# Layer 0's output projection by channel and transposed back, and its variance products spread over the MLP

## The chip, the cores and the metric

The kernel runs on one core of a Trainium2 chip. Its time is the time on the device in microseconds (us), as the median of several runs. A profile was taken of one more run. It gives for every instruction the engine, the start and the length. The engines are named as in the profile: PE is TensorE's matmul, PEld its weight load, DVE is VectorE, ACT is ScalarE, POOL is GpSimd, SP issues transfers.

## The reference, cut to what matters

The network has two layers on an image of 64 x 64 positions ("tokens") with 96 channels. Each layer is a state-space mixer with a residual, then an MLP with a residual whose values are rounded to 8-bit and 16-bit floats. The change lies where layer 0 ends. There the scan's result `y` (4096 tokens, 192 channels) is normalised over its channels, gated, projected to 96 channels and added to `x`; then comes the MLP. The tail of layer 0, with gain 1 and bias 0 of the normalisation in these inputs:

```python
y = layernorm(y, eps=1e-5) * ln_g + ln_b      # over the 192 channels of a token
y = y * silu(z)
x = x + y @ out_proj_w                        # 192 -> 96 channels, per token
# MLP
t = layernorm(x, eps=1e-5)
h = relu(q16(q8(t) @ q8(W1).T) + q8(b1))      # 96 -> 384 (each sum rounded to 16 bits)
x = x + (q16(q8(h) @ q8(W2).T) + q8(b2))      # 384 -> 96
# layer 1 begins
xn = layernorm(x, eps=1e-6);  xz = xn @ W_in.T ...
```

Since the factor 1/sqrt(variance) of a token is the same for all its channels, the kernel applies it after the projection, when it adds the result to the residual.

## The kernel before: the parts concerned

The tokens are cut into 8 chunks of 512. `res` holds the residual with tokens on the partitions (128 x 4 tokens x 96 channels of a chunk). `y` lies with channels on the partitions: `y[0]` has channels 0 to 127 of all tokens, `y[1]` has channels 128 to 191 of one chunk on partitions 0 to 63 and of another on 64 to 127 (the two `LANES`). So the work goes in turns `s` of two chunks, software-pipelined: turn `s` prepares the centred `y` of turn `s + 1`, finishes the mixer and runs the MLP for turn `s`, and hands the chunks of turn `s - 1` to layer 1.

```python
for s in range(-1, n + 1):                    # n = 4
    if s + 1 < n:
        self.centred(s + 1, chunks(s + 1))
    if 0 <= s < n:
        self.gated_out(s, chunks(s))
    for c in chunks(s - 1):
        self.to_layer1(c)
    for c in chunks(s - 1):
        self.keep_in_proj(c)
    if s + 1 < n:
        self.variance(s + 1, chunks(s + 1))
    for c in chunks(s):
        self.mlp_turn(0, c)
    for c in chunks(s):
        self.mlp_up(0, c)
    for c in chunks(s):
        self.mlp_down(0, c)
        self.xn[c] = self.norm_chunk(self.lp, c, self.eps6, F32, f"c{c}")
```

`keep` fixes an instruction's place: it stays behind all that was written before it for the same engine. All TensorE products here are kept, so TensorE works in the order of the program. What isn't kept on VectorE, ScalarE and GpSimd is put in order by the scheduler when the kernel is built. Each engine then works its own list in order.

```python
def centred(self, s, chunks):                 # subtract the mean over the channels
    m = [self.pa.tile([P, CH], F32, tag="a", name=f"m{c}") for c in chunks]
    for t, c in zip(m, chunks):
        keep(nc.tensor.matmul(t, self.mean, y0[:, chunk(c)], start=True, stop=False))
    for t, r in zip(m, LANES):
        keep(nc.tensor.matmul(t, self.mean[r], y1[r, chunk(s)], start=False, stop=True))
    ...                                       # y -= mean (VectorE), sq = y*y (ScalarE),
                                              # y *= silu(z) (GpSimd)

def variance(self, s, chunks):                # sum of squares over the channels, both chunks
    v = self.po.tile([2, CH], F32, tag="o", name=f"ov{s}")
    for i, sq in enumerate(self.sq.pop(s)):
        self.keep(nc.tensor.matmul(v, self.rows[i], sq, start=i == 0, stop=i == 2))
    sd = self.lp.tile([2, CH], F32, tag="osd", name=f"osd{s}")
    nc.scalar.activation(sd, v, AF.Sqrt, bias=self.eps5[0:2])
    r = self.lp.tile([P, 2, 4], F32, tag="or", name=f"or{s}")
    for k in range(2):
        nc.sync.dma_start(r[:, k], sd[k : k + 1].rearrange("k (p j) -> k p j", j=4))
    nc.vector.reciprocal(r, r)
    ...                                       # self.factor[c] = r[:, k]

def gated_out(self, s, chunks):
    for c in chunks:
        o = self.po.tile([P, 4, CD], F32, tag="o", name=f"o0{c}")
        self.out_proj(o, self.y, self.wg, c, self.keep)
        for j in range(4):
            to, r = self.res[:, c, j, :], self.factor[c][:, j : j + 1]
            nc.vector.scalar_tensor_tensor(to, o[:, j, :], r, to, ALU.mult, ALU.add)
        self.mlp_norm(0, c)

def out_proj(self, t, y, w, c, keep):         # L596 and L597 in the profile
    ...
    for j in range(4):                        # y stationary (128 tokens), w moves (96 columns)
        at = [slice(k * CH + j, (k + 1) * CH, 4) for k in (c, s)]
        keep(nc.tensor.matmul(t[:, j, :], y[0][:, at[0]], w[0], start=True, stop=False))
        keep(nc.tensor.matmul(t[:, j, :], y[1][r, at[1]], w[1][r], start=False, stop=True))

def to_layer1(self, c):                       # 4 transposes (L188), a ScalarE copy, a transfer
def keep_in_proj(self, c):                    # 2 products of 512 columns (L331), 2 copies
def mlp_norm(self, li, c):                    # normalise on VectorE/ScalarE, round to 8 bits,
                                              # POOL widens to bf16: xb
def mlp_turn(self, li, c):                    # 4 transposes of xb (L188), a ScalarE copy: xt
def mlp_up(self, li, c):                      # for m in 0, 1, 2:
    ...
        a = self.ph.tile([P, CH], F32, tag="h", name=f"h{li}{c}{m}")
        self.keep(nc.tensor.matmul(a, w1[:, m * P : (m + 1) * P], xt, start=True, stop=True))
        ...                                   # ScalarE copies to 16 bits, ScalarE (m = 0) or
                                              # VectorE adds b1 and clamps, POOL rounds to 8 bits
def mlp_down(self, li, c):                    # 12 products of 96 columns, then into res
```

PSUM tiles come from small pools: `a` has 3 buffers (means, input projection), `o` has 2 (out_proj, the variance, the MLP's second product), `h` has 2 (the MLP's first product), `t` has 1 (transposes).

Of the kernel before, what the change touches and what calls it, by code (L numbers as in the profile page):

```python
# [28 lines left out]
F32 = mybir.dt.float32  # L29
# [5 lines left out]
ALU = mybir.AluOpType  # L35
# [4 lines left out]
P = 128  # L40
# [3 lines left out]
CD = 96  # L44
# [4 lines left out]
CH = 512  # L49
# [44 lines left out]
LANES = (slice(0, 64), slice(64, 128))  # L94
# [12 lines left out]
def chunk(c):  # L107
    return slice(c * CH, (c + 1) * CH)
# [12 lines left out]
class Net:  # L121
# [897 lines left out]
    def back0(self):  # L1019

        tc = self.tc
        self.xn_d = self.scratch("xn1", [CD, L])
        with ExitStack() as ctx:
            self.tp = ctx.enter_context(tc.tile_pool(name="af0", bufs=3))
            self.lp = ctx.enter_context(tc.tile_pool(name="al0", bufs=2))
            self.pa = ctx.enter_context(tc.tile_pool(name="ps_a0", bufs=3, space=PSUM))  # L1030
            self.po = ctx.enter_context(tc.tile_pool(name="ps_o0", bufs=2, space=PSUM))
            self.ph = ctx.enter_context(tc.tile_pool(name="ps_h0", bufs=2, space=PSUM))
            self.pt = ctx.enter_context(tc.tile_pool(name="ps_t0", bufs=1, space=PSUM))
            self.w_in = self.w_in1
            n = NCH // 2
            self.sq, self.factor, self.xb, self.xn, self.xt, self.hid = {}, {}, {}, {}, {}, {}

            def chunks(s):
                c0 = s // 2 * 4 + s % 2
                return (c0, c0 + 2) if 0 <= s < n else ()  # L1040

            for s in range(-1, n + 1):
                if s + 1 < n:
                    self.centred(s + 1, chunks(s + 1))
                if 0 <= s < n:
                    self.gated_out(s, chunks(s))
                for c in chunks(s - 1):
                    self.to_layer1(c)
                for c in chunks(s - 1):
                    self.keep_in_proj(c)  # L1050
                if s + 1 < n:
                    self.variance(s + 1, chunks(s + 1))
                for c in chunks(s):
                    self.mlp_turn(0, c)
                for c in chunks(s):
                    self.mlp_up(0, c)
                for c in chunks(s):
                    self.mlp_down(0, c)
                    self.xn[c] = self.norm_chunk(self.lp, c, self.eps6, F32, f"c{c}")

    def keep(self, instruction):
        self.tc.keep_in_program_order(instruction)
# [20 lines left out]
    def variance(self, s, chunks):  # L1083

        nc = self.nc
        v = self.po.tile([2, CH], F32, tag="o", name=f"ov{s}")
        for i, sq in enumerate(self.sq.pop(s)):
            self.keep(nc.tensor.matmul(v, self.rows[i], sq, start=i == 0, stop=i == 2))
        sd = self.lp.tile([2, CH], F32, tag="osd", name=f"osd{s}")
        nc.scalar.activation(sd, v, AF.Sqrt, bias=self.eps5[0:2])  # L1090
        r = self.lp.tile([P, 2, 4], F32, tag="or", name=f"or{s}")
# [3 lines that stand above are left out]
        for k, c in enumerate(chunks):  # L1095
            self.factor[c] = r[:, k]

    def gated_out(self, s, chunks):

        nc = self.nc  # L1100
        for c in chunks:
            o = self.po.tile([P, 4, CD], F32, tag="o", name=f"o0{c}")
            self.out_proj(o, self.y, self.wg, c, self.keep)
            for j in range(4):
                to, r = self.res[:, c, j, :], self.factor[c][:, j : j + 1]
                nc.vector.scalar_tensor_tensor(to, o[:, j, :], r, to, ALU.mult, ALU.add)
            self.mlp_norm(0, c)

    def to_layer1(self, c):
        nc = self.nc  # L1110
# [855 lines left out]
        self.to_channels(t, self.xb.pop(c), self.identb, xt, "c (j p) -> c j p", self.keep)  # L1966
        self.xt[c] = xt

    def mlp_up(self, li, c):

        nc = self.nc
        w1, w2, b1, b2 = self.mlp_w[li]
        xt = self.xt.pop(c)
        self.hid[c] = []
        for m in range(HID // P):
            a = self.ph.tile([P, CH], F32, tag="h", name=f"h{li}{c}{m}")
            self.keep(nc.tensor.matmul(a, w1[:, m * P : (m + 1) * P], xt, start=True, stop=True))
            h16 = self.tp.tile([P, CH], F16, tag="h16", name=f"h16{li}{c}{m}")
            nc.scalar.copy(h16, a)
            if m == 0:  # L1980
                nc.scalar.activation(h16, h16, AF.Relu, bias=b1[:, m : m + 1])
            else:
                nc.vector.tensor_scalar(h16, h16, b1[:, m : m + 1], 0.0, ALU.add, ALU.max)
            h8 = self.tp.tile([P, CH], FP8, tag=f"h8{m}", name=f"h8{li}{c}{m}")
            nc.gpsimd.tensor_copy(h8, h16, saturate=False)
            self.hid[c].append(h8)
# [100 lines left out]
```

## Time and profile before

| | us |
|---|---|
| time, median of 3 runs (lowest to highest) | 1490.06 (1487.32 to 1494.84) |
| span of the profiled run | 1489.0 |
| PE busy | 1186.5 (80%) |
| DVE busy | 1155.5 (78%) |
| ACT busy | 907.6 (61%) |
| POOL busy | 784.6 (53%) |
| out_proj of layer 0, 128 records on PE | 48.6 |
| variance products, 24 records on PE | 13.5 |

Such a table says how much each engine works over the whole span, and it can mislead here: the kernel is a row of stages with different limits. The changed functions run in one stretch of some 160 us near the beginning, once per chunk or once per turn, and long before the stretch in which layer 1's scans keep VectorE busy. What a change in them is worth has to be read from that stretch: which engine works without a gap there, and what the others wait for. A product of f32 operands appears in the records as two matmuls (and two weight loads), one of 8-bit or 16-bit operands as one. The ends of matmuls are modelled, so the distance between the starts of two is the better measure of what one costs. The clock that a view gives for TensorE is the granted share of its full speed.

### The profile page before, as it was taken

The numbers are of one execution on the slowest core, as the hardware profiler recorded it, in microseconds if no ns is written. First come the engines' busy times: TensorE is split into PE (matmuls) and PEld (weight loads), VectorE is DVE, ScalarE is ACT, GpSimd is POOL, SyncE is SP. The second block draws the span as 40 slices with busy tenths as digits, with TensorE's granted clock in tenths as the row PEclk, the third lists the DMA queues.
The fourth block names the chain that finished last, engine by engine and source line by source line (L and its number), as shares of the span: only waits on it lengthen the run. The fifth ranks groups of instructions, "written<-read, shape, count | busy, mean of one in ns | idle before, by whom it ended". The sixth has DMA issues, their size and how long they took to land. (4 is left out here: it accounts for less than half of the span.)

```text
span 1489.0 us, 13012 instructions
## 1 busy us (share of the span) xinstructions
PE 1186.5 (80%) x4040; PEld 496.6 (33%) x4040; DVE 1155.5 (78%) x887; ACT 907.6 (61%) x1091; POOL 784.6 (53%) x461
## 2 busy tenths in 40 slices
PE   7998887799996377677777677787777888899975
PEld 4533444243332122222222222222222343344343
DVE  6493455303337999999999999999999999999875
ACT  3454333304446677677777777777777777777434
POOL 1002221100001687778777877777778777875545
PEclk8998566799998688888888888988888898987865
DMA  2143000003317745645555454635364557342201
GB/s 63 53 136 66 11 10 13 11 24 87 81 36 208 244 135 180 215 138 159 180 162 183 137 183 151 203 113 194 123 227 132 171 171 248 122 150 72 87 0 43
DMA packets 68851, 183.21 MB, mean 123 GB/s; under 512 B 21488, under 2 KB 35460, under 8 KB 61956
## 3 DMA queue, kind: packets, MB, share of 16 engines
q1 hardware_dynamic: 67480, 182.00, 39.3%
q8 instruction: 34, 0.56, 0.2%
q10 hardware_dynamic: 1292, 0.28, 0.1%
q14 instruction: 45, 0.37, 0.1%
HBM read 155.98 MB, written 20.47 MB: 118 GB/s over the span
## 5 line engine op out<-in xcount | busy, mean ns | idle before, releaser
L1552 POOL TENSOR_TENSOR hss<-h1s,xws 128x1024 f32<-128x1024 f32 x96 | 224.6, 2377 | 132.0 <-PE hs L1560 131.4
L1536 ACT ACTIVATE da<-dt1s,a 128x1024 f32<-128x1024 f32 x168 | 187.9, 1118 | 147.9 <-DVE xws L1547 87.5
L1560 PE MATMUL hs<-hss,ident 128*128 128x512 f32 x376 | 212.0, 647 | 59.4 <-DMA dt<-dtc 33.5
L1547 DVE TENSOR_TENSOR_SCAN xws<-da,xws 128x1024 f32<-128x1024 f32 x96 | 224.1, 2335 | 10.4 <-DVE xws L1547 2.7
L1536 ACT ACTIVATE da<-dt0s,a 128x1024 f32<-128x1024 f32 x168 | 187.2, 1114 | 68.4 <-DVE xws L1547 52.2
L1560 PE MATMUL hs<-h0s,ident 128*128 128x512 f32 x376 | 199.1, 612 | 0.0
L1547 DVE TENSOR_TENSOR_SCAN h1s<-da,h1s,xws 128x1024 f32<-128x1024 f32 x72 | 169.2, 2350 | 10.4 <-ACT da L1536 1.3
L1560 PEld LDWEIGHTS hs<-hss,ident 128*128 128x128 f32 x376 | 68.6, 200 | 193.4 <-issue 75.9
L1375 POOL TENSOR_TENSOR dun<-u,dtn 128x512 f32<-128x512 f32 x4 | 5.9, 1482 | 197.8 <-DVE dtn L1272 107.6
L1560 PEld LDWEIGHTS hs<-h0s,ident 128*128 128x128 f32 x376 | 74.1, 198 | 97.2 <-issue 92.4
L1581 PE MATMUL acc<-hc2s,fold 128*32 128x512 f32 x128 | 47.1, 825 | 61.0 <-POOL hc2s L1570 58.0
L1581 PE MATMUL acc<-hc0s,fold 128*32 128x512 f32 x128 | 46.2, 809 | 52.6 <-POOL hc0s L1570 52.6
L1581 PE MATMUL acc<-hc1s,fold 128*32 128x512 f32 x128 | 46.5, 815 | 50.1 <-POOL hc1s L1570 50.1
L1520 POOL TENSOR_TENSOR x1s<-x1s,dus 128x1024 f32<-128x1024 f32 x32 | 75.0, 2361 | 8.8 <-DMA x1s<-bc 8.8
L1520 POOL TENSOR_TENSOR x2s<-x2s,dus 128x1024 f32<-128x1024 f32 x32 | 75.3, 2369 | 6.9 <-DMA c1s<-bc 6.9
L1547 DVE TENSOR_TENSOR_SCAN x0s<-da,x0s 128x1024 f32<-128x1024 f32 x32 | 74.7, 2335 | 4.3 <-ACT da L1536 2.0
L1547 DVE TENSOR_TENSOR_SCAN x1s<-da,x1s 128x1024 f32<-128x1024 f32 x32 | 74.7, 2335 | 3.5 <-ACT da L1536 0.9
L1547 DVE TENSOR_TENSOR_SCAN x2s<-da,x2s 128x1024 f32<-128x1024 f32 x32 | 74.7, 2335 | 3.4 <-ACT da L1536 0.8
L1560 PE MATMUL hs<-x0s,ident 128*128 128x512 f32 x128 | 66.7, 603 | 0.2 <-DVE x0s L1547 0.2
L1560 PE MATMUL hs<-x1s,ident 128*128 128x512 f32 x128 | 66.6, 602 | 0.0
L1520 POOL TENSOR_TENSOR x0s<-x0s,dus 128x1024 f32<-128x1024 f32 x28 | 65.8, 2363 | 0.0
L1232 PE MATMUL cv<-pad,cw 128*128 128x512 f32 x144 | 64.3, 598 | 0.0
(343 smaller groups left out, 2423.1 us busy)
## 6 DMA issues: line engine op xcount, KB each, us to landing
c0s<-bc SPq DMA_DIRECT2D x184, 128.0 KB, 2.6
c1s<-bc SPq DMA_DIRECT2D x184, 128.0 KB, 2.6
x2s<-bc SPq DMA_DIRECT2D x32, 512.0 KB, 4.8
x0s<-bc SPq DMA_DIRECT2D x28, 512.0 KB, 3.8
x1s<-bc SPq DMA_DIRECT2D x28, 512.0 KB, 6.2
dus<-du SPq DMA_DIRECT2D x20, 512.0 KB, 6.7
dt1s<-dt SPq DMA_DIRECT2D x40, 256.0 KB, 6.6
dt0s<-dt SPq DMA_DIRECT2D x40, 256.0 KB, 4.6
```

What stands on the lines that cost most here:

```text
L1232: keep(nc.tensor.matmul(t, cw[0][:, tap, 0:P], v, start=tap == 0, stop=False))
L1375: keep(nc.gpsimd.tensor_tensor(dun, u[1][:, m], dtn, ALU.mult))
L1520: keep(nc.gpsimd.tensor_tensor(x, x, du[:, part[j]], ALU.mult))
L1536: keep(nc.scalar.activation(das[i, s], dts[o][:, part[j]], AF.Exp, scale=self.a6[:, g, k : k + 1]))
L1547: keep(nc.vector.tensor_tensor_scan(to, da, x, start, ALU.mult, ALU.add))
L1552: keep(nc.gpsimd.tensor_tensor(cols(hs)[:, w, :], grid(h1)[:, w, :], grid(xw)[:, w, :], ALU.add))
L1560: keep(nc.tensor.matmul(t, self.ident, x[:, chunk(m)], start=x is hs, stop=x is xs[i % 3]))
L1581: keep(nc.tensor.matmul(to, self.fold4, src, start=k == 0, stop=k == NK - 1))
```

## The change

`gated_out` used `y` as the stationary operand: for each 128 tokens it loaded 128 columns of `y` and moved only the 96 columns of the weights through the array. Now the weights are stationary, and 512 tokens move in one product. The result then has channels on the partitions. ScalarE copies it out of PSUM, and four transposes per chunk bring it back to tokens, where the factor is applied as before. The layer-1 transposes of the turn before are put between the two chunks' transposes. The second part concerns the variance of the next turn: its three products no longer stand in one block ahead of the MLP. One comes before the MLP, and one in each chunk's `mlp_up` ahead of the last of three products. The MLP's transposes and first products go chunk by chunk, where both chunks were transposed first before.

```diff
                 if 0 <= s < n:
-                    self.gated_out(s, chunks(s))
-                for c in chunks(s - 1):
-                    self.to_layer1(c)
+                    self.gated_sums(s, chunks(s))
+                for k in range(2):
+                    for c in chunks(s - 1)[k : k + 1]:
+                        self.to_layer1(c)
+                    for c in chunks(s)[k : k + 1]:
+                        self.gated_out(c)
                 for c in chunks(s - 1):
                     self.keep_in_proj(c)
-                if s + 1 < n:
-                    self.variance(s + 1, chunks(s + 1))
+                sums = self.variance(s + 1, chunks(s + 1)) if s + 1 < n else iter(())
+                next(sums, None)
                 for c in chunks(s):
                     self.mlp_turn(0, c)
-                for c in chunks(s):
-                    self.mlp_up(0, c)
+                    self.mlp_up(0, c, lambda: next(sums, None))
+                for _ in sums:
+                    pass
...
         for i, sq in enumerate(self.sq.pop(s)):
             self.keep(nc.tensor.matmul(v, self.rows[i], sq, start=i == 0, stop=i == 2))
+            if i < 2:
+                yield
...
+    def gated_sums(self, s, chunks):
+        nc, keep = self.nc, self.keep
+        o = [self.ph.tile([P, CH], F32, tag="h", name=f"oc{c}")[0:CD] for c in chunks]
+        for t, c in zip(o, chunks):
+            keep(nc.tensor.matmul(t, self.wg[0], self.y[0][:, chunk(c)], start=True, stop=False))
+        for t, r in zip(o, LANES):
+            keep(nc.tensor.matmul(t, self.wg[1][r], self.y[1][r, chunk(s)], start=False, stop=True))
+        self.ot = {}
+        for t, c in zip(o, chunks):
+            self.ot[c] = self.lp.tile([CD, CH], F32, tag="ot", name=f"ot{c}")
+            nc.scalar.copy(self.ot[c], t)

-    def gated_out(self, s, chunks):
+    def gated_out(self, c):
         nc = self.nc
-        for c in chunks:
-            o = self.po.tile([P, 4, CD], F32, tag="o", name=f"o0{c}")
-            self.out_proj(o, self.y, self.wg, c, self.keep)
-            for j in range(4):
-                ...
-            self.mlp_norm(0, c)
+        o = self.po.tile([P, 4, CD], F32, tag="o", name=f"o0{c}")
+        by_token = self.ot[c].rearrange("c (p j) -> c j p", j=4)
+        for j in range(4):
+            self.keep(nc.tensor.transpose(o[:, j, :], by_token[:, j, :], self.ident[0:CD, 0:CD]))
+        for j in range(4):
+            ...                               # as before
+        self.mlp_norm(0, c)
...
-    def mlp_up(self, li, c):
+    def mlp_up(self, li, c, between=lambda: None):
...
         for m in range(HID // P):
+            if m == 2:
+                between()
```

More of the change, by code (lines that the diff above doesn't have):

```diff
@@ L1096, in variance @@
             self.factor[c] = r[:, k]
-    def gated_out(self, s, chunks):
-        nc = self.nc
-        for c in chunks:
-            o = self.po.tile([P, 4, CD], F32, tag="o", name=f"o0{c}")
-            self.out_proj(o, self.y, self.wg, c, self.keep)
-            for j in range(4):
-                to, r = self.res[:, c, j, :], self.factor[c][:, j : j + 1]
-                nc.vector.scalar_tensor_tensor(to, o[:, j, :], r, to, ALU.mult, ALU.add)
-            self.mlp_norm(0, c)
+    def gated_sums(self, s, chunks):
[10 more added lines that the diff above has]
+    def gated_out(self, c):
+        nc = self.nc
+        o = self.po.tile([P, 4, CD], F32, tag="o", name=f"o0{c}")
[3 more added lines that the diff above has]
+        for j in range(4):
+            to, r = self.res[:, c, j, :], self.factor[c][:, j : j + 1]
+            nc.vector.scalar_tensor_tensor(to, o[:, j, :], r, to, ALU.mult, ALU.add)
+        self.mlp_norm(0, c)
     def to_layer1(self, c):
```

## The prediction

> **What bounds the kernel now.** I first asked where the change sits in the span: the rows of its lines place it between 124.6 and 284.6 us of 1489, in the stretch where layer 0 is finished and its MLP runs. From the page's slices, each 37.2 us, the clock row matters most here:
>
> ```profile
> PE   7998887799996377677777677787777888899975
> PEclk8998566799998688888888888988888898987865
> ```
>
> The fifth to seventh slices (149 to 261 us) have TensorE 70 to 80% busy at 0.5 to 0.7 of its clock, the lowest in the kernel. Then I cut the stretch at the starts of its pipeline turns, in the windows view (us, busy time and number of records of PE, PEld, DVE, ACT, POOL, then clock, DMA share, GB/s):
>
> ```profile
> 133.80:164.30 30.50, 25.20 (x85) 13.47 (x85) 12.91 (x31) 10.81 (x21) 9.32 (x12) 0.69 0.04 6
> 164.30:202.10 37.80, 31.60 (x103) 17.09 (x102) 18.71 (x44) 14.13 (x28) 8.73 (x11) 0.68 0.04 11
> 202.10:240.10 38.00, 31.56 (x103) 17.12 (x102) 18.74 (x44) 14.12 (x28) 8.74 (x11) 0.68 0.04 11
> 240.10:270.60 30.50, 23.97 (x89) 14.96 (x87) 16.21 (x39) 11.76 (x24) 4.78 (x8) 0.61 0.06 14
> 284.60:400.00 115.40, 115.40 (x480) 41.56 (x480) 27.02 (x42) 36.88 (x52) 2.54 (x2) 1.00 0.21 58
> ```
>
> The first four rows are turns s = 0 to 3. No engine but TensorE is busy even half of a turn, and it is busy 83% of it. The last row is layer 1's convolution, which begins when the last turn's input projection is copied: TensorE is busy in every microsecond of it, so whatever the turns lose or win moves the rest of the kernel by as much. Next, the inside of turn 1, cut at its steps: the means, out_proj, the transposes to layer 1, its input projection, the variance, the wait for the normalised rows, and the MLP:
>
> ```profile
> 164.30:169.70 5.40, 5.40 (x11) 1.67 (x9) 3.25 (x8) 1.82 (x4) 0.00 (x0) 0.52 0.02 3
> 169.70:180.80 11.10, 11.10 (x35) 8.69 (x33) 5.02 (x12) 1.56 (x3) 2.53 (x2) 0.64 0.00 0
> 180.80:183.20 2.40, 1.73 (x9) 1.25 (x9) 1.92 (x6) 1.11 (x2) 0.12 (x1) 0.50 0.00 0
> 183.20:188.40 5.20, 5.20 (x10) 2.12 (x8) 1.54 (x3) 2.27 (x5) 1.14 (x1) 0.68 0.26 76
> 188.40:191.10 2.70, 2.70 (x7) 0.42 (x6) 1.99 (x6) 0.63 (x2) 0.67 (x1) 1.00 0.00 0
> 191.10:194.30 3.20, 0.65 (x8) 0.47 (x8) 1.06 (x3) 1.34 (x3) 0.51 (x1) 1.00 0.04 1
> 194.30:202.10 7.80, 4.82 (x34) 2.46 (x33) 3.93 (x8) 5.39 (x10) 3.76 (x6) 0.66 0.00 0
> ```
>
> out_proj is the largest step, 11.1 us, and weight loads are 8.7 us of it. Up to 191 TensorE has no gap over 1 us: it sets the time. From 191 on it waits on others, first for normalised rows (0.65 of 3.20 us busy), then for the MLP's copies. Last, single rows of the timeline (start, length, engine, line, shapes):
>
> ```profile
> 164.33 3.75 PE L1070 MATMUL m<-y,mean 128*128 128x512 f32 x4
> 168.01 1.82 PE L1072 MATMUL m<-y,mean 64*128 64x512 f32 x4
> 169.75 0.71 PE L596 MATMUL o<-wg,y 128*128 128x96 f32 x2
> 175.08 0.78 PE L596 MATMUL o<-wg,y 128*128 128x96 f32 x2
> 180.76 1.09 PE L188 MATMUL tr<-ident,lnxnc 128*96 128x128 f32 x4
> 188.47 2.74 PE L1088 MATMUL ov<-sq,rows 128*2 128x512 f32 x6
> 194.11 0.42 PE L188 MATMUL tf<-identb,xb 128*96 128x128 bf16 x4 [2.55 <-POOL xb L1960]
> ```
>
> One f32 product is two records. Two out_proj records start every 0.64 us at the beginning and every 0.71 us later, after the clock has fallen: it is bound by the loads, not by the stream. A transpose is one record of 0.27 us. A 512-column record takes 0.85 us at the half clock (the variance of turn 0: six in 5.05 us) and 0.43 at the full one (six here in 2.67 us). The last row: the second chunk's turn waits 2.55 us for POOL, while the first chunk could already go through the MLP.
>
> **What the Trainium skill says.** "TensorE: Matmul & The Clock Gate", Part 1: the clock is halved by default and goes up after a window of about 3.4 us of activity. The trace agrees: the means start at 0.85 us a record, and 3.7 us later the rate has doubled. It also shows what I don't find there: out_proj, without a gap, lets the clock fall again (1.00 to 0.50 near 173 us). Part 4 of that page says that transposes don't count as activity for the clock. No row here isolates that. Part 3 says that products in different row groups run together: agrees, four 64-row records of the means take 1.74 us from start to start against 3.68 for four 128-row ones, although the clock rose between. "ScalarE: Activation LUTs", What ACT_TABLE_LOAD costs, has 0.833 ns per element plus a fixed part. The trace has 0.58 us for a copy of 512 columns (96 rows), the size of each added copy.
>
> **The change, part by part**, for turns 1 and 2.
>
> (a) Removed: 16 products of 96 columns, 32 records, 169.75 to 180.76: −11.0 us.
>
> (b) Added: four products of 512 columns. Two have 128 rows (4 records) and two have 64 rows in different row groups, which run as one (2 record times). So 6 record times: 2.6 us at the full clock, 5.1 at the half. They directly follow 5.4 us of means, at whose end the clock is full, so I take 3.0.
>
> (c) Added: 8 transposes back to tokens, 8 × 0.27 = 2.2, and 0.3 more because their stationary side has 128 columns and is read with a step of four: 2.5 us.
>
> (d) Added: two ScalarE copies of 0.58 us. TensorE must wait for them, but the layer-1 transposes (1.1 us a chunk) lie between. Those in turn had a wait of 0.67 us for their single PSUM buffer, which the new transposes fill. I take both as zero.
>
> (e) Moved: of the variance's 2.67 us a third stays in line, 0.9. The rest goes between MLP products that wait for ScalarE: −1.8 us.
>
> Before the first chunk's turn: −11.0 + 3.0 + 2.5 − 1.8 = −7.3 us. The turn then begins 26.8 − 7.3 = 19.5 us after the means. Are its rows there? The first chunk's transposes end some 10.6 us after the means' start (5.4 + 3.0 + 1.1 + 1.1). The additions (4 × 0.31), three VectorE passes of 0.55, ScalarE's square 0.52 and root 0.30, reciprocal 0.17, product 0.55, POOL's 0.5 and handovers make about 5.5 us: ready near 16 to 17.5. So yes, with 2 us to spare.
>
> (f) Turn and first MLP part go chunk by chunk. From the first turn to the means it was 10.9 us (191.14 to 202.06). ScalarE needs there 2 × 0.57 for copies, 6 × 0.585 and 2 × 0.73 for the activations, 6.1 us, and now the variance's root of 0.68, which used to lie in the wait. With the ramp (1.5) and the last chunk's down products (2) I come to about 10.2: −0.7 us.
>
> So some 8 us a turn at best. For the order in which ScalarE and VectorE are now queued I take 1.5 off: 6.5 a turn, 13 for two.
>
> Turn 0 has no layer-1 work to hide behind. After its 3.0 us of means: 3.0 of products, about 1 exposed for a copy, 2.5 of transposes; the first rows are ready some 13.5 us into the turn and its end comes near 24.5 to 25.5. It was 30.5: −5.5. Turn 3 has no means ahead of it, so its products run at the half clock (5.1); then transposes 4.7, projection 5.1 to 6 and MLP 9.5, about 25 against 30.5: −5.
>
> Sum: 13 + 5.5 + 5 = 23.5 us. The opening (124.6 to 133.8) and the last 14 us (270.6 to 284.6) are untouched.
>
> **The rivals.**
> 1. The chain of the normalised rows takes the place of the products. The trace has a bad sign: in turn 1 the first chunk's products end at 175.2 but its rows reach TensorE at 191. In between ScalarE's square starts only at 185.84, behind a pad copy which waits for TensorE. Queues are served in order; if the new order repeats that, each turn keeps 3 to 4 us of wait: −10 in all, 1480.
> 2. The half clock holds on, since transposes don't warm the array: (b) costs 5.1 and the variance's share 1.7. Then turns 1 and 2 win 4.5 each: −17, 1473. Against it: the means warm the clock in both turns.
> 3. The opposite: dense 512-column streams keep the full clock through projection (5.07 to 3.4 us) and variance, and every wait for rows vanishes: 9 us in turns 1 and 2, 7 in the others: −32, 1458.
> 4. The gain is hidden anyway: if layer 1's convolution waited for a transfer or for POOL, nothing would move. Its row speaks against this: no idle at all, and its weights were asked for at 125 to 128 us.
>
> **Range and chances.** From −23.5 I take 3.5 more for rival 1, the likeliest: −20, so 1470 us. The range, 1459 to 1481, spans rivals 3 and 1. For a gain over 2% the time must be under 1460.3, about rival 3 in full: 0.1. For a loss over 2% some 50 us would have to be lost in a stretch of 160: 0.02.
>
> **What would show each step.** Turns of 30 to 31 us in place of 37.8 and 38.0, and of 25 in place of 30.5. The row of the sums four products at about 0.43 us a record time (half clock: 0.85). The 32 new transposes at 0.27 to 0.31 us. The variance no longer in one block, and MLP products not later for it. The second chunk's wait on POOL below 1 us. The convolution beginning near 265 us instead of 284.6, and no different after that. I am wrong if the first turn of the rows waits long on POOL (rival 1), if ScalarE's copies stand late in its queue so that TensorE waits for the transposes' input, or if the time after the convolution's start changes by more than 3 us.

## The result, and the profile after

The changed kernel takes 1452.54 us (median of 4 runs, 1447.18 to 1458.65), before 1492.45 (4 runs, 1487.32 to 1496.37): ratio 0.9736, 95% interval 0.9684 to 0.9788. That is twice the gain I had predicted, and below my range. The page's rows for TensorE and its clock in 40 slices, now 36.3 us each:

```profile
PE   7997777999981677787776776677778888899875
PEclk8999886999995889888888988878889998978855
```

The slices with the lowest clock, the fifth to seventh, now show 0.8, 0.8 and 0.6, where they showed 0.5, 0.6 and 0.6. The windows view of the changed kernel, cut at the starts of turns 0 to 3, the last stretch (ahead of layer 1's convolution), and the convolution, with the columns as before:

```profile
132.70:157.80 25.10, 17.82 (x69) 5.63 (x69) 11.79 (x30) 11.90 (x23) 9.45 (x12) 0.73 0.04 5
157.80:181.70 23.90, 18.34 (x90) 7.38 (x86) 18.67 (x44) 14.82 (x30) 8.86 (x11) 1.00 0.07 17
181.70:207.20 25.50, 20.50 (x88) 8.03 (x86) 19.29 (x44) 14.72 (x30) 8.85 (x11) 0.91 0.06 17
207.20:233.40 26.20, 18.76 (x73) 8.72 (x70) 16.48 (x40) 12.55 (x26) 4.95 (x8) 0.70 0.07 16
233.40:246.90 13.50, 7.57 (x20) 3.55 (x19) 6.21 (x14) 4.46 (x9) 0.00 (x0) 0.61 0.10 29
246.90:362.30 115.40, 115.40 (x480) 41.53 (x480) 27.02 (x42) 36.87 (x52) 2.54 (x2) 1.00 0.22 60
```

All of the gain lies in the stretch from the first means to the convolution: 160.0 us before (124.6 to 284.6), 123.4 now (123.5 to 246.9). From the convolution's start to the end it was 1204.4 us and is 1205.2. Turns 1 and 2 gave most: 37.8 and 38.0 us became 23.9 and 25.5. Their clock was 0.68 and is 1.00 and 0.91. Turn 1 from inside, cut at means, sums, both kinds of transposes, layer 1's projection, the first variance product, the wait for rows, and the MLP:

```profile
157.80:160.70 2.90, 2.90 (x13) 0.96 (x9) 2.66 (x7) 1.00 (x2) 0.00 (x0) 1.00 0.00 0
160.70:163.60 2.90, 2.90 (x10) 0.82 (x8) 2.90 (x7) 1.75 (x4) 0.59 (x1) 1.00 0.00 0
163.60:167.00 3.40, 2.32 (x18) 1.83 (x17) 3.30 (x10) 2.90 (x6) 2.28 (x3) 1.00 0.03 10
167.00:170.60 3.60, 3.60 (x10) 1.41 (x9) 3.43 (x10) 2.15 (x5) 0.94 (x1) 1.00 0.37 105
170.60:171.50 0.90, 0.90 (x3) 0.09 (x2) 0.90 (x3) 0.00 (x0) 0.00 (x0) 1.00 0.00 0
171.50:172.30 0.80, 0.13 (x1) 0.00 (x0) 0.80 (x2) 0.28 (x1) 0.67 (x1) 1.00 0.00 0
172.30:181.70 9.40, 5.59 (x43) 2.27 (x43) 4.68 (x11) 6.74 (x14) 4.38 (x7) 1.00 0.01 0
```

The steps that the diff touches are shorter, but so are two that it does not touch: the means (5.4 us before, 2.9 now) and the projection to layer 1 (5.2, now 3.6). The clock column says why. The single rows of the timeline that answer to those of before:

```profile
157.82 1.95 PE L1075 MATMUL m<-y,mean 128*128 128x512 f32 x4
160.76 1.96 PE L1110 MATMUL oc<-y,wg 128*96 128x512 f32 x4
163.68 0.64 PE L188 MATMUL tr<-ident,lnxnc 128*96 128x128 f32 x4
164.41 0.72 PE L1124 MATMUL o<-ident,ot 96*128 96x96 f32 x4
167.05 3.63 PE L331 MATMUL in<-xt,w_in 96*128 96x512 f32 x8
172.34 0.42 PE L188 MATMUL tf<-identb,xb 128*96 128x128 bf16 x4 [0.71 <-POOL xb L1981]
```

Four transposes now take 0.64 us where they took 1.09. Here TensorE waits 0.71 us for the first chunk's rows, and no row of this turn shows a wait for the second chunk's.

### The profile page after: what moved, and what is told of

Read it like the earlier page. It is cut to its first block, busy times and chain, and to the rows that moved or that the text cites. A ratio compares the mean times of both kernels' runs of the same rounds, so it can differ in the third digit from the quotient of the medians.

```text
span 1452.1 us, 12894 instructions
## 1 busy us (share of the span) xinstructions
PE 1153.0 (79%) x3976; PEld 465.0 (32%) x3976; DVE 1154.9 (80%) x887; ACT 909.9 (63%) x1099; POOL 785.6 (54%) x461
## 5 line engine op out<-in xcount | busy, mean ns | idle before, releaser
L1581 PE MATMUL hs<-h0s,ident 128*128 128x512 f32 x376 | 203.2, 623 | 0.3 <-DVE h0s L1568 0.3
L1568 DVE TENSOR_TENSOR_SCAN h1s<-da,h1s,xws 128x1024 f32<-128x1024 f32 x72 | 169.2, 2350 | 10.9 <-ACT da L1557 2.2
L1396 POOL TENSOR_TENSOR dun<-u,dtn 128x512 f32<-128x512 f32 x4 | 5.9, 1480 | 197.2 <-DVE dtn L1293 107.6
```

The lines of the kernel that those rows point to most:

```text
L1396: keep(nc.gpsimd.tensor_tensor(dun, u[1][:, m], dtn, ALU.mult))
L1568: keep(nc.vector.tensor_tensor_scan(to, da, x, start, ALU.mult, ALU.add))
L1581: keep(nc.tensor.matmul(t, self.ident, x[:, chunk(m)], start=x is hs, stop=x is xs[i % 3]))
```

## The experiments

Two theories to begin with. **Theory 1:** the old 96-column products let the clock fall, and the new 512-column ones hold it. **Theory 2:** the clock fell in the MLP's waits, and the spread variance products keep the array awake there. The table has the time of each kernel (median), its ratio to the kernel before with the 95% interval, and from its one profile the length of the stretch, of turns 0 to 3, and the clock in turns 1 and 2. Two profiles of the same kernel differ by some us in the stretch (the changed kernel: 123.4 and 119.2). The time from the program's start to the first means also varied, from 119 to 133 us among the profiles. So the stretch tells more than the total. Time and ratio of r2 leave out one of its runs, of 1472.71 us, in which the clock was lower throughout.

| kernel | us | ratio (interval) | stretch | turns 0 to 3 | clock 1, 2 |
|---|---|---|---|---|---|
| before | 1492.45 | | 160.0 | 30.5, 37.8, 38.0, 30.5 | 0.68, 0.68 |
| changed | 1452.54 | 0.9736 (0.9684 to 0.9788) | 123.4 | 25.1, 23.9, 25.5, 26.2 | 1.00, 0.91 |
| changed, again (r1) | 1452.93 | 0.9750 (0.9714 to 0.9785) | 119.2 | 24.3, 23.9, 23.7, 24.0 | 1.00, 1.00 |
| e1 | 1463.31 | 0.9828 (0.9774 to 0.9882) | 132.4 | 24.7, 27.1, 27.4, 29.5 | 0.82, 0.81 |
| e2 | 1475.38 | 0.9893 (0.9851 to 0.9935) | 152.3 | 30.3, 33.2, 34.3, 30.8 | 0.79, 0.80 |
| e3 | 1452.12 | 0.9771 (0.9702 to 0.9839) | 124.8 | 24.3, 28.7, 24.7, 23.3 | 0.81, 0.94 |
| e4 | 1458.47 | 0.9796 (0.9756 to 0.9836) | 129.2 | 26.7, 25.8, 24.8, 28.2 | 0.95, 1.00 |
| e5 | 1480.06 | 0.9925 (0.9875 to 0.9975) | 149.8 | 25.0, 33.3, 37.0, 31.0 | 0.70, 0.64 |
| e6 | 1441.68 | 0.9645 (0.9603 to 0.9687) | 113.6 | 22.8, 25.2, 23.8, 21.5 | 0.94, 1.00 |
| e7 | 1457.60 | 0.9753 (0.9714 to 0.9792) | 122.6 | 22.9, 25.8, 26.8, 24.7 | 0.90, 0.82 |
| e7, again (r2) | 1458.99 | 0.9758 (0.9719 to 0.9796) | 123.1 | 22.8, 26.3, 26.8, 24.7 | 0.82, 0.82 |
| e8 | 1461.70 | 0.9798 (0.9738 to 0.9858) | 130.5 | 25.1, 26.4, 28.1, 28.7 | 0.87, 0.88 |
| e8, again (r3) | 1468.66 | 0.9823 (0.9788 to 0.9858) | 133.2 | 24.3, 30.9, 29.5, 26.2 | 0.78, 0.83 |
| e9 | 1498.82 | 1.0054 (1.0032 to 1.0076) | 167.2 | 30.4, 40.0, 35.9, 37.5 | 0.76, 0.88 |
| e10 | 1476.32 | 0.9896 (0.9825 to 0.9967) | 149.0 | 26.7, 32.7, 31.8, 34.1 | 0.87, 0.88 |
| e11 | 1461.47 | 0.9767 (0.9695 to 0.9838) | 125.1 | 24.3, 26.0, 25.4, 26.0 | 0.87, 1.00 |

**e1: only the projection by channel.**

```diff
-                sums = self.variance(...) if s + 1 < n else iter(())
-                next(sums, None)
+                for _ in self.variance(...) if s + 1 < n else ():
+                    pass
                 for c in chunks(s):
                     self.mlp_turn(0, c)
-                    self.mlp_up(0, c, lambda: next(sums, None))
-                for _ in sums:
-                    pass
+                for c in chunks(s):
+                    self.mlp_up(0, c)
```

> The changed kernel with the variance and the MLP's order as before: only the output projection by channel is left. Theory 1 (the old 96-column products let TensorE's clock fall, the new 512-column ones hold it): the clock of turns 1 and 2 stays above 0.9, the turns take 26 to 27 us, the kernel about 1460 us. Theory 2 (the spread variance products fill the MLP's waits and so hold the clock up to the next means): turns 1 and 2 fall to a clock of 0.7 to 0.8 and take 30 to 31 us, the kernel about 1472 us.

Measured: a clock of 0.82 and 0.81, turns of 27.1 and 27.4, between the two. Two rows of turn 2's timeline say where each theory holds:

```profile
181.72 3.75 PE L1074 MATMUL m<-y,mean 128*128 128x512 f32 x4
192.94 3.62 PE L331 MATMUL in<-xt,w_in 96*128 96x512 f32 x8
```

The means still start at the half clock (3.75 us for four records), so theory 2 is right about the start of a turn. From then on the clock is full, and layer 1's projection takes 3.62 us: theory 1 is right about the rest. In these profiles the projection by channel alone brings 27.6 of the 36.6 us.

**e2: only the spread products and the MLP by chunk**, with the old projection.

```diff
                 if 0 <= s < n:
-                    self.gated_sums(s, chunks(s))
-                for k in range(2):
-                    ...                       # to_layer1 and gated_out in turns
+                    self.gated_old(s, chunks(s))   # the old gated_out with out_proj
+                for c in chunks(s - 1):
+                    self.to_layer1(c)
```

> The old projection of 96-column products, with the variance products spread and the MLP chunk by chunk. Theory 1: the clock of turns 1 and 2 stays near 0.7 as before, each turn wins about 2 us, the kernel about 1484 us. Theory 2: the means start at the full clock, the clock is about 0.85, each turn wins 4 to 5 us, the kernel about 1475 us.

Measured: 0.79 and 0.80, turns 4.6 and 3.7 us shorter. Turn 1 in the timeline:

```profile
173.74 1.95 PE L1072 MATMUL m<-y,mean 128*128 128x512 f32 x4
190.32 5.19 PE L331 MATMUL in<-xt,w_in 96*128 96x512 f32 x8
```

Now the means are at the full clock and layer 1's projection is not. In this turn it is the mirror image of e1; in turn 2 the means begin at the half clock again (3.55 us). The stretch is 7.7 us shorter; with e1's 27.6 that makes 35.3 of 36.6, so the two parts add up, within what two profiles of one kernel differ by. This profile was of a run with a long opening (1487.64 us); the kernel's other three runs took 1471.05 to 1476.98.

**e3: the new products in pieces of 128 columns.**

```diff
-            keep(nc.tensor.matmul(t, self.wg[0], self.y[0][:, chunk(c)], ...))
+            for q in range(4):
+                at = slice(c * CH + q * P, c * CH + (q + 1) * P)
+                keep(nc.tensor.matmul(t[:, q * P : (q + 1) * P], self.wg[0], self.y[0][:, at], ...))
```

and the 64-row products likewise.

> The changed kernel with each product of 512 columns of the new projection cut into four of 128 columns with the same weights, loaded anew each time: 32 records a turn as in the old projection, and the same columns in all. Theory 1 in its form 'a stream of short products with a load each lets the clock fall': the clock of turns 1 and 2 falls below 0.8, the turns take 29 us or more, the kernel 1465 to 1470 us. If the clock depends on the waits alone (theory 2): the clock stays at 0.95, only the sums grow from 2.9 to 5 or 6 us a turn, the kernel about 1463 us.

Measured: neither. 16 records of 128 columns took 1.99 us, as 4 records of 512 did (1.96); the loads of 96 columns vanish behind the moving ones. The time is that of the changed kernel. In turn 1 layer 1's projection ran at the half clock (6.85 us, after a stretch of transposes), in turn 2 at the full one (3.63). So neither the number of products nor that of loads is what cost.

**e4: e1 with an idle product in each chunk's first MLP part.**

```diff
+    def idle_product(self):
+        t = self.pa.tile([P, CH], F32, tag="a", name="idle")
+        v = self.cw1[0].rearrange("p a b -> p (a b)")[:, 0:CH]
+        self.keep(self.nc.tensor.matmul(t[0:2], self.rows[0], v, start=True, stop=True))
...
-                    self.mlp_up(0, c)
+                    self.mlp_up(0, c, self.idle_product)
```

> The projection by channel alone, variance in its block, and one idle product of 512 columns in each chunk's first MLP part, where the spread variance would stand; its result is not used. Theory 1: as the run without the idle products, within 3 us. Theory 2: the clock of turns 1 and 2 is higher than there by 0.15 or more, the turns are 3 us shorter, the kernel about 6 us faster than that run although TensorE has more to do.

Measured: 0.95 and 1.00, turns of 25.8 and 24.8 instead of 27.1 and 27.4, although TensorE does more. The shortening is 1.3 and 2.6 us where I expected 3. The means of turns 1 and 2, which took 3.75 us each in e1:

```profile
157.05 3.30 PE L1074 MATMUL m<-y,mean 128*128 128x512 f32 x4
182.87 1.95 PE L1074 MATMUL m<-y,mean 128*128 128x512 f32 x4
```

In turn 2 theory 2's mechanism is shown: columns moved in the MLP's waits kept the next means at the full clock. Ahead of turn 1 they did not suffice.

**e5: the old kernel with stationary tokens in a row.** The result lands at other tokens than in the reference; all else is the old kernel.

```diff
-            at = [slice(k * CH + j, (k + 1) * CH, 4) for k in (c, s)]
+            at = [slice(k * CH + j * P, k * CH + (j + 1) * P) for k in (c, s)]
```

> The kernel before, with the stationary operand of the old projection read as 128 tokens in a row instead of every fourth one; the result lands at other tokens than in the reference, the amount of work is the same. Theory O (the orientation itself is dear: 128 columns to load for 96 that move): a record stays at 0.32 to 0.36 us, loads at 0.33, the projection at 11 us a turn, the time within 5 us of before. Theory S (the step of four makes the loads slow): loads fall to about 0.19 us as those of the means' weights, the projection to 6 or 7 us a turn, the kernel to 1470 to 1475 us.

Measured: the loads of the old projection, from its row in the kernel before and then in e5 (minimum, median, maximum in ns):

```profile
L596 PEld LDWEIGHTS o<-wg,y x64: 308/329/332, 136.8 to 250.2; 128*128 128x128 f32 x64
```

```profile
L596 PEld LDWEIGHTS o<-wg,y x64: 186/189/333, 135.9 to 237.7; 128*128 128x128 f32 x64
```

At the full clock the step of four is what makes a load slow: with unit step two records start every 0.39 us instead of 0.64, and the projection takes 6.6 us in turn 0. So theory S is right about the size. But the time, 1480, missed what it expected. In turn 0 the clock falls near 141.5 us, 5.6 us after the projection began; in turn 2 near 199.5. A record then costs 0.335 us (0.355 with the step of four). Turn 0 is as short as in the changed kernel (25.0), turn 2 hardly shorter than before (37.0).

**e6: the changed kernel with idle products in the remaining waits.**

```diff
                 for k in range(2):
+                    if s == 3:
+                        self.idle_product(2 - k)
+                    if s == 4 and k == 0:
+                        self.idle_product(4)
...
                 next(sums, None)
+                if s == 0:
+                    self.idle_product(2)
...
-                    self.mlp_up(0, c, lambda: next(sums, None))
+                    self.mlp_up(0, c, self.idle_product if s == 3 else lambda: next(sums, None))
```

> The changed kernel with idle products of 512 columns in the waits where TensorE still falls to the half clock: two in turn 0 ahead of the MLP, in turn 3 three around the transposes and one in each chunk's first MLP part, four ahead of the last transposes. If the clock is what those stretches lose: turn 3 at 22 to 23 us instead of 26.2, the last stretch at 11.5 to 12 instead of 13.5, the kernel 5 to 8 us faster than the changed one, about 1446 us. If the waits for VectorE and ScalarE set the time there: no gain, or 2 us slower, 1452 to 1455 us.

Turn 3 and the last stretch of e6 in the windows view:

```profile
202.80:224.30 21.50, 16.98 (x85) 6.70 (x83) 16.48 (x40) 12.40 (x26) 4.96 (x8) 1.00 0.08 19
224.30:235.50 11.20, 8.51 (x27) 2.87 (x26) 6.55 (x14) 4.40 (x9) 0.00 (x0) 1.00 0.14 36
```

The clock is 1.00 where it was 0.70 and 0.61, and the two stretches take 21.5 and 11.2 us instead of 26.2 and 13.5 (24.0 and 14.1 in r1). The gain, 10.9 us, is above the expected 5 to 8. This is the fastest kernel of the study: 1441.68 us, with an interval (0.9603 to 0.9687) below that of the changed kernel's larger set of runs (0.9714 to 0.9785). Its extra products compute nothing.

**e7: the variance in its block, the MLP by chunk**; run twice (again as r2).

```diff
-                next(sums, None)
+                for _ in sums: pass           # all three products here
                 for c in chunks(s):
                     self.mlp_turn(0, c)
-                    self.mlp_up(0, c, lambda: next(sums, None))
+                    self.mlp_up(0, c)
```

> The changed kernel with the variance in its block ahead of the MLP, but the MLP still chunk by chunk. If the order by chunk brings what the second part of the change wins: within 2 us of the changed kernel. If the spread products bring it, through the clock: the means of turns 1 and 2 start at the half clock, the stretch is 7 to 9 us longer than in the changed kernel, as with the projection alone.

> The variance in a block, the MLP by chunk, once more. If the order by chunk alone brings what the second part wins: within 2 us of the changed kernel in the stretch and in the time. If the spread products bring some of it by holding the clock: 3 to 6 us slower, with the means of turns 1 and 2 at the half clock in most of their records.

> The changed kernel once more, beside the two below on one chip, since single profiles of the stretch differ by some us with the phase of the clock. Both theories: the stretch of 123 us again within 4 us, the time 1452 within 5 us.

Measured: stretches of 122.6 and 123.1, against 123.4 and 119.2 of the changed kernel and 132.4 of e1. Over the whole stretch the order by chunk thus brings most of what the second part wins, but 6.0 of its 9.6 us lie behind turn 2 (turn 3 and the last stretch), against a single profile of e1. In turns 1 and 2 it is the other way round: together they take 54.5 us in e1, 52.9 on average here and 48.5 in the changed kernel. So there the order brings 1.6 us and the spread 4.4, through the clock: without the spread the means of both turns begin at the half clock in both profiles (2.94 to 3.68 us for four records), with it in one turn of four (3.09). The spread costs some of this again in turn 0 (24.7 against 22.9). The medians differ by 5 and 6 us, but the intervals on one chip overlap (0.9719 to 0.9796 and 0.9714 to 0.9785). What the spread wins in the whole kernel stays open; the stretch says 1.5 us.

**e8: the two kinds of transposes not in turns**; run twice (again as r3).

```diff
-                for k in range(2):
-                    for c in chunks(s - 1)[k : k + 1]:
-                        self.to_layer1(c)
-                    for c in chunks(s)[k : k + 1]:
-                        self.gated_out(c)
+                for c in chunks(s - 1):
+                    self.to_layer1(c)
+                for c in chunks(s):
+                    self.gated_out(c)
```

> The changed kernel with the layer-1 transposes of both chunks first and the new transposes of both chunks after them. If putting them in turns hides the copies: 0.7 to 1 us more a turn in turns 1 to 3, the stretch 2 to 3 us longer. If ScalarE's order hides them anyway: no difference beyond 1 us.

> The transposes not put in turns, once more. If the wait for the single PSUM buffer and for the copies costs what its first profile showed: 5 to 9 us slower than the changed kernel. If that profile was an unlucky phase of the clock: 1 to 3 us.

Measured: stretches of 130.5 and 133.2, so 10.6 us more than the changed kernel's on average, and a median 15.7 us above it in r3. Both expectations put it too low. Turn 1 of r3:

```profile
172.46 0.64 PE L188 MATMUL tr<-ident,lnxnc 128*96 128x128 f32 x4 [1.58 <-ACT xt L189]
173.94 6.87 PE L331 MATMUL in<-xt,w_in 96*128 96x512 f32 x8
```

The added wait is 0.6 us more than in the changed kernel (1.58 against 0.98), but behind it layer 1's projection runs at the half clock: 6.87 us instead of 3.63. So it does in turn 2 of r3 (6.73) and of e8 (5.87). In turn 1 of e8 the clock held (3.62) in spite of a wait of 1.80.

**e9: the old projection with four idle products a turn inside it.**

```diff
             keep(nc.tensor.matmul(t[:, j, :], y[1][r, at[1]], w[1][r], ...))
+            if j % 2:
+                between()                     # one idle product of 512 columns
```

> The kernel before with one idle product of 512 columns behind every second group of the old projection, four a turn, 3.4 us of added work at the full clock. If the old products let the clock fall because their columns keep the array busy for only a quarter of the time: the clock stays full through the projection, the transposes and layer 1's input projection (that one 3.6 us instead of 5.1, the transposes 0.64 instead of 1.09 us a chunk), it is 0.8 in turns 1 and 2 instead of 0.68, and the turns are no longer than 38.5 us. If the fall has another cause, such as the loads with a step of four: the clock falls in the projection as before and the turns take 41 to 44 us.

Measured: both. In turn 2 the clock held and the turn took 35.9 us with its added work, less than the 38.0 without it. It held through the projection of turn 0 too. In turn 1 it fell 8 us after the means, and the turn took 40.0. Turn 3 had the half clock throughout its projection and took 37.5 instead of 30.5, and the kernel is 0.5% slower. Undecided by itself; the loads with a step of four were the same in all turns, so they alone do not make it fall.

**e10: the edits of e9 and e5 together.** Again the result lands at other tokens.

> The kernel before with unit-step loads (the result lands at other tokens) and, inside the old projection, four idle products of 512 columns a turn. If the share of time in which columns move decides (estimate: 0.41 with unit step alone, 0.44 with idle products alone, 0.6 with both): the clock holds from the means to the variance in turns 1 and 2, transposes at 0.64 us a chunk, layer 1's projection at 3.6 us, the two turns 32 to 34 us in spite of the added work. If not the share but the kind of product decides: the clock falls within 8 us of the means as with unit step alone, and the turns take 36 to 39 us.

```profile
187.60 3.58 PE L1072 MATMUL m<-y,mean 128*128 128x512 f32 x4
202.20 0.64 PE L188 MATMUL tr<-ident,lnxnc 128*96 128x128 f32 x4
204.00 3.60 PE L331 MATMUL in<-xt,w_in 96*128 96x512 f32 x8
```

Measured: the clock held from the end of the means to the variance in both turns, which took 32.7 and 31.8 us. Only the means still began at the half clock (3.58 us in turn 2). e5, with four products fewer a turn, took 33.3 and 37.0. So the old kind of product does not bring the clock down by itself; a stream in which columns move too seldom does. As an estimate from the traces: 512 columns take 0.43 us at the full clock, so 96 take 0.08; the old records start every 0.32 us (a share of 0.25), those of e5 every 0.195 (0.41), those of e3 move 0.11 us in every 0.12 (0.9). With idle products between, e9 comes to 0.44 and e10 to 0.62. The clock fell at 0.25 and 0.41, in one of the three turns that met 0.44 at the full clock, and held at 0.62 and above.

The granted clock of all sixteen profiles shows more. It is either full or half, and it changes only at points that lie whole multiples of 3.41 us apart. I mean by a piece such an interval of 3.41 us, and reckon the share of moved columns for each from about 119 us to the convolution (again an estimate; records of 16 or 8 bits take half as long). In all 97 pieces after which the clock fell the share was at most 0.52. In all 270 after which it stayed full the share was at least 0.38. Getting it up is another matter: in all 97 pieces after which it rose the share was some 0.75 or more. But 15 of the 186 after which it stayed half had that too; 13 of these hold transposes, against 17 of the 97. So in turn 3 of e10 the stream began at the half clock and stayed there for 18 us with a share of 0.67 (at half the clock 96 columns take 0.16 us), which would have held a full clock. Why those 15 brought no rise stays open.

**e11: e8 with two idle products between the layer-1 transposes of the two chunks.**

```diff
-                for c in chunks(s - 1):
+                for k, c in enumerate(chunks(s - 1)):
+                    if k:
+                        self.idle_product(2)
                     self.to_layer1(c)
```

> The changed kernel with the transposes not in turns, as before, and two idle products of 512 columns between the layer-1 transposes of the two chunks, where TensorE waits for the copy. If the clock's fall after a stretch of transposes is what cost there: layer 1's projection at 3.6 us in turns 1 and 2, turns of 24 to 26 us, the stretch 122 to 126 us. If the wait itself cost: turns of 26 to 31 us as without the idle products, the stretch above 130 us.

Measured: layer 1's projection at 3.6 us in turns 1, 2 and 3, turns of 26.0 and 25.4, the stretch 125.1. The time of the kernel does not show it: 1461.47 us, with an interval (0.9695 to 0.9838) that overlaps those of e8 and r3. By the profiles, what putting the transposes in turns brings is mostly the clock: it shortens the time without moving columns to what the clock survives.

## Why the prediction was wrong

The bound was named rightly, TensorE's own list in these turns, and so was the place: nothing after the convolution's start changed. Turns 0 and 3 came near (−5.4 and −4.3 us, predicted −5.5 and −5; −6.2 and −6.5 in r1). Turns 1 and 2 won 13.9 and 12.5 us where I had 6.5 each, and the difference of 13.4 is what the sum of 23.5 lacked. The stretch as a whole won 36.6. For turn 1, by the prediction's steps:

| step | predicted us | measured us |
|---|---|---|
| means (left as they were) | 0 | −2.5 |
| (a), (b) products | −8.0 | −8.1 |
| (c), (d) transposes and their waits | +2.5 | +0.7 |
| layer 1's projection (left as it was) | 0 | −1.5 |
| (e) variance and the wait for the first rows | −1.8 | −0.9 |
| (f) from the first turn of rows to the next means | −0.7 | −1.6 |
| queue order (taken off) | +1.5 | 0 |

**The step that failed** is the sum "before the first chunk's turn". It priced everything but the new products as in the old trace: means at the half clock, transposes at 0.27 us, projection at 5.07 us. I had seen that out_proj lets the clock fall while it works without a gap. I did not conclude that to remove out_proj is to remove the cause of the half clock in all that follows it. Rival 3 said this of projection and variance, though not of the means, with 32 us, and got a chance of 0.1. e1, e2 and e4 show the two halves: without the old projection the clock stays full through the rest of the turn (e1), and with the MLP's waits filled it can be full at the turn's start (in turn 1 of e2, in turn 2 of e4). e5 and e10, with the count over all profiles, show that it is the share of moved columns. Turn 1 won 7.4 us more than forecast. Means, transposes with their waits, and projection are 5.8 of them, and the 1.5 taken off for the queue order most of the rest.

Point by point besides. (b) was right to 0.1 us. Of (a) I had the size and the bound, the loads, but not what made the loads slow: at the full clock it is their step of four (e5). (d) was right that the copies of the sums are hidden. The wait for the single PSUM buffer did not vanish (0.98 us, before 0.67), and what the interleaving buys is mostly the clock (e8, e11). Rival 1 did not come: TensorE waits 0.71 us for the first chunk's rows. ScalarE's square stands behind a pad copy again, but that copy waits for a projection which now takes 3.6 us. (f) was undersized: −1.6 us, with no wait left for the second chunk's rows. The spread was priced as TensorE time moved into waits (e); that its columns keep the clock up for the next means, which e7 shows, stood in no term. Rival 2, the half clock holding on, is what e8 shows to be near: one more wait among the transposes brought it in three of four turns.

I misread some lines of the old trace. The clock did not rise during the means of turn 1: it is 0.50 from 166.0 to 169.4 us and full only just before out_proj. What looked like a doubled rate at 168.0 is the 64-row products going in pairs. So these rows show the pairing without the clock's help, and the full clock that (b) counted on rested on a rise only 0.3 us ahead of out_proj. In turn 3 VectorE is busy for 16.21 of 30.50 us, more than half. And a transpose was priced at the length of its record, 0.27 us, whose end is modelled; from start to start it took 0.22 at the half clock and takes 0.12 at the full one.

For e6, "TensorE: Matmul & The Clock Gate" of the Trainium skill, in Why this matters for your kernels, asks that TensorE have no gap over some 3 us. The first means of the changed kernel agree: a gap of 3.22 us stands ahead of them, and the clock is full until 0.8 us after their start and then half. The gap of 4.38 us in the last stretch shows nothing of this, as the clock was at the half when it began. And the old projection lost the clock without any gap, so a stream has to be dense as well as unbroken.

## What to carry to other kernels

When a change takes a stream of short, load-bound products out of a stage, price the rest of the stage at the clock it will then have. The clock row by stage, and where in the stage it falls, say what that is. To hold the clock, look at the share of time in which columns move, not only at gaps: put real products into waits, and where there are none, idle products in a wait cost little and brought 6 to 10 us of the stretch here (123.4 or 119.2 to 113.6). If a stationary operand is f32 and read with a step, try the same with unit step before judging the orientation.

## What the runs showed of the hardware that I had not expected

- The clock falls during continuous work: 5.6 us after the projection of 96-column products began in e5's turn 0. It also falls after about 3.7 us of transposes with one wait of 1.58 us in them (r3), and the next dense work then ran at half speed nearly throughout (6.87 us for 8 records).
- In the old projection a load of 128 f32 columns takes 189 ns at the full clock with unit step and 329 with a step of four; at the half clock up to 333 with unit step, so there the step costs hardly more.
- Products of 128 columns, each with its 96 columns of weights loaded anew, are as fast as products of 512 (16 records in 1.99 us, 4 in 1.96).
- f32 transposes follow the clock: four in 0.64 us at the full one, in 1.09 at the half. Part 4 of the page named above says that transposes don't engage the full clock. The pieces that brought no rise (13 of 15 with transposes) fit this. But once it is engaged by other products they run at it, and they can hold it. In turn 2 of the changed kernel the first of these two pieces has almost nothing but transposes (0.44 of an estimated share of 0.51), and the clock stayed full behind it:

```profile
189.19:192.58 3.39, 2.53 (x19) 2.10 (x18) 2.79 (x9) 3.08 (x6) 1.88 (x2) 1.00 0.11 28
192.60:196.00 3.40, 3.40 (x9) 1.23 (x8) 3.25 (x9) 1.86 (x5) 0.64 (x1) 1.00 0.28 86
```
